# Half of an output projection moved from its own stage into the attention loop

## The chip, the core and the metric

The kernel runs on one core of a Trainium2 chip. Its time is the device time of one execution in microseconds; before the change it was 3228.24, 3230.65 and 3234.8 us in three runs, 3230.65 in the median. Five engines work side by side, each through its own queue in order: TensorE (PE, with the loading of its weights shown as PEld), VectorE (DVE), ScalarE (ACT), GpSimd (POOL) and SyncE (SP), which here issues nearly all transfers. Results of TensorE go to PSUM and are read from there by VectorE and ScalarE.

## What is computed

Two layers on `x` of 2 x 1024 tokens of width 512. The change concerns the first layer's attention, a gated delta rule with 16 heads of width 128, and above all its last line, the output projection with `Wo` of 2048 x 512:

```python
def step(S, inps):
    qt, kt, vt, at, bt = inps
    Sk = jnp.einsum('bhvk,bhk->bhv', S, kt)
    err = Sk - vt
    S = at[..., None, None] * S - bt[..., None, None] * (err[..., None] * kt[:, :, None, :])
    ot = jnp.einsum('bhvk,bhk->bhv', S, qt)
    return (S, ot)
...
o = (o - mu) * jax.lax.rsqrt(var + 1e-05) * ln_w + ln_b
g = jax.nn.sigmoid(x @ Wg).reshape(B, T, H, DV)
o = (o * g).reshape(B, T, H * DV)
return o @ Wo
```

Around it:

```python
xn = _layernorm(x, axis=-1)
s = _L0_attn_ref(xn, ...)
g = _silu(_L0_ffn_ref(xn, ...))
x = x + s * g
xn = _layernorm(x, axis=-1)
```

The second layer is a gated recurrence over the tokens and an MLP with packed 4-bit weights, which ends in another `x + s * g`. All products are in float32 or close to it.

## The kernel before, in words

Time goes through four stages. A front computes the first layernorm, the first MLP (its result `gd` goes to HBM) and prepares the keys of the first head groups (0 to 436 us). Then comes the **attention loop** (436 to about 1798 us), then the **join** (the rest of the output projection, the gate, the sum and the second layernorm, to 2024 us), then the second layer.

**The loop.** Tokens are cut into `NC` = 8 chunks of 128 and heads into `HG` = 8 groups of two; with both batch entries a group has `NS` = 4 streams. A unit is one chunk of one head group. `units` takes the groups in pairs: units 0 to 15 are groups 0 and 1 in turn, 16 to 31 groups 2 and 3, and so on to 63. So heads 0 to 7 are finished for all chunks soon after unit 31.

A unit's own work is a chain of short dependent steps. `across` solves a triangular system in four blocks: a product into `zw`, a copy (`w4`), four small transfers of 16 KB (`wt`), then the next block; at its end it updates the state (`pst`). `finish` makes the unit's output (`po`), normalises, gates it and stores it (`od<-ot`) in HBM. Beside the chain, `weave` hands out wide products in portions by their costs in `LINKS` = 10 links a unit. These are projections for later windows: `made` for queries, values and gates, and `ahead_k` for keys, three groups ahead. Each is eight products of 128x512 (`WIDE`). Chains of neighbouring units overlap: `weave` gets the chain of the unit before and that of this unit, and advances one in each link. `later(n, ...)` defers the steps that follow a product by n links.

With `turn4` = u % 4, a unit with turn4 2 or 3 carries two such projections. One with turn4 0 or 1 carries one and, while `slot + 3 < HG`, `ahead_k` as a second; from unit 40 on there are no keys left to make, and these are the light units.

**Order.** In the loop the compute engines keep the program's order (`Ordered`). The transfers on SP, and all that the join issues, are placed by a scheduler when the program is built. SP executes its queue in order, and a transfer that waits holds up those behind it.

**The join.** `Join` is made by `then()` at unit 48 (slot `HG - 2`), after the pools of the loop's key side are closed (`early`: `at_a`, `at_k`, `at_l`). Its constructor loads all of `Wo` in four transfers of 1 MB (L154). `order` lists the 16 tiles of 128 tokens by chunk, then batch entry; a tile is named by its place i there, 0 to 15. `load_o` (L174) loads a tile's heads, 1 MB, `load_xg` its `x` and `gd`. `product` multiplies the 16 heads into one PSUM tile `jpo`; `rest` gates it (L216), adds `x` (L212), stores it (`x1d`), takes statistics (L207 to L209), a power on GpSimd (L219) and normalises (L220). `turn` transposes the tile twice (`ptr`, L114), once into `xd` in HBM through ScalarE, once into the operand `xq` of the second layer through VectorE, with four differences for odd chunks.

Tiles 0 to 2 are multiplied in the loop's last two passes and after it. `run` makes the other 13: it starts a tile's product, turns the former tile after 8 of its 16 heads, and does the rest. The second layer's first weights are unpacked on VectorE in the same stretch, since the scheduler lets them in as soon as their room is free.

Of the kernel before, what the change touches and what calls it, by code (L numbers as in the profile page):

```python
# [13 lines left out]
F32 = mybir.dt.float32  # L14
# [4 lines left out]
ALU = mybir.AluOpType  # L19
# [3 lines left out]
P = 128  # L23
B, T, D = 2, 1024, 512
NT = B * T
KC = D // P
NTT = NT // P
H = 16
HG = H // 2
NC = T // P  # L30
NS = 4
# [32 lines left out]
def done(steps):  # L64
    for _ in steps:
        pass
# [56 lines left out]
class Ordered:  # L123


    def __init__(self, tc, engine, on):
        self.tc, self.engine, self.on = tc, engine, on
# [11 lines left out]
class Join:  # L139
# [1 line left out]

    def __init__(self, tc, a, cst, minus_half, od, gd, x1d):
        self.tc, self.a, self.cst, self.minus_half = tc, a, cst, minus_half
        self.od, self.gd, self.x1d = od, gd, x1d
        self.ctx = ExitStack()
        self.tp = [self.pool("j_t", 1)]
        wp, self.op = self.pool("j_w", 1), [self.pool("j_o", 1)]
        self.lp = self.pool("j_ln", 3)  # L150
        self.wo = []
        for h0 in range(0, H, 4):
            w = wp.tile([P, 4, D], F32, name=f"wo_{h0}")
            tc.nc.sync.dma_start(  # L154
                w, a["wo"][h0 * P : (h0 + 4) * P, :].rearrange("(h p) e -> p h e", p=P)
            )
            self.wo += [w[:, h, :] for h in range(4)]
        self.order = [(c, b) for c in range(NC) for b in range(B)]
        self.o, self.xg, self.made = [], [], 0
        self.load_xg()  # L160

    def pool(self, name, bufs):
        return self.ctx.enter_context(self.tc.tile_pool(name=name, bufs=bufs, reuse_waits="tile"))

    def more_room(self):
        self.tp.append(self.pool("j_t2", 2))
# [2 lines left out]
    def load_o(self):  # L169

        n = len(self.o)
        c, b = self.order[n]
        ot = self.op[n % 3 > 0].tile([P, H, P], F32, tag="ot", name=f"jo_{b * NC + c}")
        self.tc.nc.sync.dma_start(ot, self.od[c].rearrange("p (h b) t -> p b h t", b=B)[:, b])  # L174
        self.o.append(ot)

    def load_xg(self):
# [10 lines left out]
    def product(self, psp, tag, matmul):  # L188


        nc = self.tc.nc
        i = self.made
        self.made += 1
        c, b = self.order[i]
        ti = b * NC + c
        ot, (xt, g) = self.o[i], self.xg[i]
        po = psp.tile([P, D], F32, tag=tag, name=f"jpo_{ti}")
        for h in range(H):
            matmul(po, lhsT=ot[:, h, :], rhs=self.wo[h], start=(h == 0), stop=(h == H - 1))  # L199
            if h == H - 1:  # L200
                st, mv, ve, rs = (
                    self.lp.tile([P, n], F32, tag=f"ln_{t}", name=f"ln_{t}")
                    for t, n in (("st", 6), ("mv", 2), ("ve", 1), ("rs", 1))
                )

                def stats():
                    nc.vector.bn_stats(st, xt)  # L207
                    nc.vector.bn_aggr(mv, st)
                    nc.vector.tensor_scalar(ve, mv[:, 1:2], EPS, None, ALU.add)  # L209

                def added():
                    nc.vector.tensor_tensor(xt, g, xt, ALU.add)  # L212
                    nc.sync.dma_start(self.x1d[ti], xt)

                self.rest = lambda out=g: (
                    lambda: nc.vector.tensor_tensor(g, po, g, ALU.mult),  # L216
                    added,
                    stats,
                    lambda: nc.gpsimd.tensor_tensor(rs, ve, self.minus_half[:, 0:1], ALU.pow),  # L219
                    lambda: nc.vector.tensor_scalar(  # L220
                        out, xt, mv[:, 0:1], rs, ALU.subtract, ALU.mult
                    ),
                )
            yield WIDE

    def run(self, xd, xq, xp):

        nc, tc = self.tc.nc, self.tc
        with self.ctx as ctx:
            ps_o, ps_t = (  # L230
                ctx.enter_context(tc.tile_pool(name=n, bufs=bufs, space=PSUM, reuse_waits="tile"))
                for n, bufs in (("j_pso", 3), ("j_pst", 2))
            )
            late = None
            for i in range(NTT):
                if i >= self.made:
                    for _ in range(min(i + 3, NTT) - len(self.o)):
                        self.load_o()
                    product = self.product(ps_o, "pso", nc.tensor.matmul)
                    done(itertools.islice(product, H // 2))  # L240
                    if late is not None:
                        late(nc, ps_t, "pst", self.xg[i - 1][0].rearrange("p (k t) -> p k t", k=KC))
                    done(product)
                    g = self.xg[i][1]
                    if i == NTT - 1:
                        g = xp.tile([P, D], F32, name="xn_last")
                    for step in self.rest(g):
                        step()
                elif late is not None:
                    late(nc, ps_t, "pst", self.xg[i - 1][0].rearrange("p (k t) -> p k t", k=KC))  # L250
                if late is not None:
                    for _ in range(min(i + 3, NTT) - len(self.xg)):
                        self.load_xg()
                g = g if i == NTT - 1 else self.xg[i][1]
                late = functools.partial(self.turn, xd, xq, *self.order[i], g)
        return late
# [14 lines left out]


@with_exitstack
def first_layer(ctx, tc, a, cst, minus_half, keep, xnT, od, gd, then):

# [24 lines left out]
    nc = tc.nc  # L302
# [7 lines left out]
    pools = {}  # L310
# [215 lines left out]
    def later(n, *steps):  # L526


        for i, step in enumerate(steps):
            if order["loop"] and n + i:  # L530
                due.setdefault(order["slot"] + n + i, []).append(step)
            else:
                step()
# [85 lines left out]
    def ahead_k(hg, p, wk, store):  # L619
        ka = pa.tile([P, NS, 2 * P], F32, tag="ka", name=f"ka_{hg}_{p}")  # L620
        store["ka", p] = ka
        yield from project(1, "wk", hg, p, wk, ka)
        later(5, lambda: nc.sync.dma_start(store["k"][p], ka))
# [341 lines left out]
    with tc.issue_after(last["act"].ins):  # L965
# [3 lines left out]
        done(made(0, 0, "v"))  # L969
        done(made(1, 0, "q"))  # L970
        done(within(0, 0, stores[0]))
        def joined():

            for cost in joining.product(pools["a"], "pa", PE.matmul):
                yield cost
            later(1, *joining.rest())
# [3 lines left out]
        for u in range(len(units) + 1):  # L980
# [15 lines left out]
            if u % 8 == 0:  # L996
                steps = invert(slot + 2, stores[slot + 2]) if slot + 2 < HG else none
                if slot + 3 < HG:
                    wk = load_weights(slot + 3, ("wk",))
                    stores[slot + 3] = new_store(slot + 3)  # L1000
                if slot == HG - 2:
                    early.close()
                    joining = then()
            if u % 8 < 7:
                for k in (0, 2, 4, 5, 7, 9) if u % 8 else (0, 7, 8, 9):
                    later(k + 1, lambda steps=steps: next(steps, None))
            pot, late = late, none
            other(pot, 1, 8 * NARROW)
            later(8, lambda pot=pot: done(pot))
# [21 lines left out]
            if turn4 < 2:  # L1031
                if slot + 3 < HG and u < len(units):
                    tail = [(ahead_k(slot + 3, i, wk["wk"], stores[slot + 3]), 8 * WIDE)]
            elif turn4 == 2:
                if u < len(units):
                    tail = [(made(C, p, "gate"), 8 * WIDE)]
            elif p + 1 < NP:
                tail = [(made(C, p + 1, "q"), 8 * WIDE)]
            elif C + 2 < HG:
                tail = [(made(C + 2, 0, "q"), 8 * WIDE)]  # L1040
# [23 lines left out]
            for hg, n, when in (  # L1064
# [2 lines left out]
            ):  # L1067
                if at == when and hg < HG:
                    weights.setdefault(hg, {}).update(load_weights(hg, ("w" + n,)))
            if joining and at == 8:  # L1070
                joining.load_o()
            if u == len(units) - 2:

                last_w.close()
                joining.more_room()
                for _ in range(2):
                    joining.load_o()
                    joining.load_xg()
# [433 lines left out]
def body(ctx, tc, a, out):  # L1512
# [7 lines left out]
    od = [tc.dram_tile([P, H * B, P], F32, name=f"od_{c}") for c in range(NC)]  # L1520
    x1d = [tc.dram_tile([P, D], F32, name=f"x1d_{ti}") for ti in range(NTT)]
    xd = [tc.dram_tile([KC, P, T], F32, name=f"xd_{b}") for b in range(B)]

    xp = ctx.enter_context(ExitStack())

    xnT = xp.enter_context(tc.tile_pool(name="xn", bufs=1)).tile([P, KC, B, T], F32, name="xnT")
    joining = first_layer(
        tc, a, cst, minus_half, keep, xnT, od, gd, lambda: Join(tc, a, cst, minus_half, od, gd, x1d)
    )
    eo = ctx.enter_context(tc.tile_pool(name="eo", bufs=1, side="right", reuse_waits="tile"))  # L1530

# [78 lines left out]
```

## Time and profile before

| what | value |
|---|---|
| runs | 3228.24, 3230.65, 3234.8 us |
| profiled execution | 3230.2 us, span 3228.4 us, mean granted clock 0.994 |
| loop, unit 0 to the end of unit 62 | 436.5 to 1777.8 us |
| wide products in units 44 to 57 | 162 |
| output projection `jpo` | 256 products: 48 by L131 in and just after the loop, 208 by L199 |
| `wo` in 4 transfers | issued 1479.7 to 1489.6, 5.7 to 10.2 us to landing |
| `jo` in 16 transfers | 6.1 us to landing, median |
| `jx`, `jg`, `xd`, `x1d` in the join's steady part | 2.7, 3.0, 3.3, 5.2 us to landing |

A product of float32 is shown as two records, so 256 products are 512 records of `jpo`. In the profile `po<-w_d` belongs to the second layer. The rows of the profile quoted later name an engine, a line of the kernel, an operation and its output and inputs; in windows, each engine has its busy time and its count of instructions, and then follow the granted clock of TensorE as a share, the mean busy share of the 16 DMA engines and the rate in GB/s.

### The profile page before, as it was taken

What the parts mean: (1) busy time and instruction counts of PE and PEld (TensorE: products, weight loads), DVE (VectorE), ACT (ScalarE), POOL (GpSimd) and SP (SyncE); (2) the same over time, 40 slices, a digit from 0 to 9 for tenths busy, and PEclk for the clock granted to TensorE, in tenths of its full rate; (3) what the DMA queues carried; (4) which work ended last, traced back from release to release, by engine and by line L of the source; (5) the groups of instructions that cost most, each with busy time, mean ns of one, the idle gap of its engine ahead of it and who ended that gap; (6) DMA issues with size and microseconds to landing.
All of it is one profiled execution on the core that took longest, in us unless ns stands there. A gap on an engine that the chain in (4) does not pass through costs nothing.

```text
span 3228.4 us, 38168 instructions
## 1 busy us (share of the span) xinstructions
PE 3162.7 (98%) x12454; PEld 1958.0 (61%) x12454; DVE 2145.3 (66%) x4286; ACT 1245.8 (39%) x2259; POOL 829.7 (26%) x1204
## 2 busy tenths in 40 slices
PE   8999999999999999998999999999999999999998
PEld 6566756666666666665666544555555555555554
DVE  4566578686877877675655433676677666776677
ACT  3475445546555555444444100222222222322223
POOL 2000022322222232222332200333323332333322
PEclk9999999999999999999999999999999999999999
DMA  6244333444434443434323544111001010110014
GB/s 181 65 140 108 97 109 107 116 129 129 122 109 132 134 127 110 98 112 130 88 71 85 165 136 120 39 33 33 26 26 33 27 33 27 33 33 27 26 36 130
DMA packets 498246, 281.11 MB, mean 87 GB/s; under 512 B 206848, under 2 KB 443136, under 8 KB 498048
## 3 DMA queue, kind: packets, MB, share of 16 engines
q1 hardware_dynamic: 490048, 265.83, 29.3%
q0 software_dynamic: 5696, 8.65, 1.0%
q10 hardware_dynamic: 2304, 4.20, 0.4%
q8 instruction: 99, 1.62, 0.2%
q14 instruction: 99, 0.81, 0.1%
HBM read 179.71 MB, written 86.25 MB: 82 GB/s over the span
## 4 chain that ended last, share of the span: by engine, by line
PE 85%; DVE 5%; DMA 3%; issue 3%; ACT 2%; SPq 1%; POOL 1%; DVEq 0%; ACTq 0%; POOLq 0%
PE po L131 15%; PE pua L131 7%; PE pga L131 7%; PE pgate L131 6%; PE pwk L131 6%; PE pwq L131 5%; PE jpo L199 5%; PE pwv L131 4%; PE zw L131 4%; PE pgc L131 3%; PE puc L131 3%; PE pg L403 2%; PE pu L403 2%; PE po L426 2%; PE pub L131 2%
## 5 line engine op out<-in xcount | busy, mean ns | idle before, releaser
L131 DVE TENSOR_TENSOR acc<-acc,po 128x512 f32<-128x512 f32 x408 | 278.2, 682 | 208.3 <-PE po L131 207.6
L131 PEld LDWEIGHTS po<-w_d,i 128*128 128x128 f32 x1024 | 194.5, 190 | 142.6 <-issue 110.7
L131 PE MATMUL po<-w_d,i 128*128 128x256 f32 (+1 forms) x1024 | 275.3, 392 | 0.0
L131 PE MATMUL pgate<-xnT,wg 128*128 128x512 f32 x512 | 248.6, 595 | 0.0
L131 PE MATMUL pwv<-xnT,wv 128*128 128x512 f32 x512 | 245.0, 593 | 1.8 <-ACT gate L131 1.8
L131 PE MATMUL pwq<-xnT,wq 128*128 128x512 f32 x512 | 245.2, 593 | 0.0
L131 PE MATMUL pua<-xq,w_u 128*128 128x512 f32 x512 | 240.6, 592 | 0.0
L131 PE MATMUL pga<-xq,w_g 128*128 128x512 f32 x512 | 240.6, 592 | 0.0
L131 PE MATMUL pwk<-xnT,wk 128*128 128x512 f32 x512 | 236.8, 593 | 2.4 <-ACT ka L131 2.4
L131 ACT COPY g<-pga 128x512 f32<-128x512 f32 x96 | 56.2, 585 | 447.2 <-PE pga L131 440.0
L131 DVE SCALAR_TENSOR_TENSOR v<-prewv,cw,v 128x512 f32<-128x512 f32 x192 | 168.2, 877 | 64.6 <-ACT v L131 53.1
L131 PEld LDWEIGHTS po<-w_d,s 128*128 128x128 f32 x720 | 136.8, 190 | 95.4 <-issue 77.3
L131 PE MATMUL po<-w_d,s 128*128 128x256 f32 x720 | 184.8, 379 | 0.0
L199 PE MATMUL jpo<-wo,jo 128*128 128x512 f32 x416 | 182.9, 597 | 0.0
L131 ACT COPY w<-zw 128x128 f32<-128x128 f32 x192 | 50.6, 264 | 338.9 <-PE zw L131 338.6
L131 POOL TENSOR_TENSOR rs<-rs,minus_half 128x4 f32<-128x4 f32 x64 | 64.4, 1007 | 426.9 <-DVE rs L131 387.9
L131 DVE SCALAR_TENSOR_TENSOR ka<-prewk,cw,ka 128x512 f32<-128x512 f32 x192 | 148.1, 773 | 37.1 <-ACT ka L131 26.7
L131 PEld LDWEIGHTS zw<-rr,ground 128*128 128x128 f32 x512 | 97.1, 193 | 123.7 <-issue 98.0
L131 DVE TENSOR_TENSOR rr<-rr,zw 128x128 f32<-128x128 f32 x192 | 54.9, 286 | 175.8 <-PE zw L131 174.2
L131 DVE SCALAR_TENSOR_TENSOR q<-prewq,cw,q 128x512 f32<-128x512 f32 x192 | 159.3, 830 | 14.4 <-ACT q L131 8.0
L131 POOL TENSOR_TENSOR ot<-ot,gate 128x512 f32<-128x512 f32 x64 | 87.1, 1360 | 297.5 <-ACT ot L131 266.6
L131 ACT ACT_TABLE_LOAD x115 | 147.5, 1283 | 14.5 <-PE pr L131 11.3
(244 smaller groups left out, 6612.9 us busy)
## 6 DMA issues: line engine op xcount, KB each, us to landing
e<-gr SPq DMA_DIRECT2D x64, 256.0 KB, 4.1
de<-e SPq DMA_DIRECT2D x64, 256.0 KB, 2.7
dk<-ka SPq DMA_DIRECT2D x32, 512.0 KB, 2.8
kb<-dk SPq DMA_DIRECT2D x64, 256.0 KB, 3.5
eb<-de SPq DMA_DIRECT2D x64, 256.0 KB, 3.0
eg<-egr SPq DMA_DIRECT2D x64, 256.0 KB, 3.9
od<-ot SPq DMA_DIRECT2D x64, 256.0 KB, 2.1
jo<-od SPq DMA_DIRECT2D x16, 1024.0 KB, 6.1
```

Of the source, the lines that this page charges most:

```text
L131: i = getattr(self.engine, name)(*args, **kw)
L199: matmul(po, lhsT=ot[:, h, :], rhs=self.wo[h], start=(h == 0), stop=(h == H - 1))
L403: nc.tensor.matmul(pp, lhsT=mw[wt, ic][:, kc, :], rhs=part, start=(kc == 0 and i == 0), stop=(kc == KC - 1 and i == 1),)
L426: nc.tensor.matmul(po[tl], lhsT=part[:, tl * P : (tl + 1) * P], rhs=mw["dwT", ic - 1], start=(ic == 1 and i == 0), stop=(ic == IC and i == 1),
```

## The change

For 8 of the 16 tiles (4, 5, 7, 8, 10, 11, 12 and 13) the first eight heads are multiplied in the loop, in the second place of the light units 44, 45, 48, 49, 52, 53, 56 and 57. The eight heads' part of `Wo` is loaded in units 41 to 43 into buffers of the key side that are free by then (`woh`: two of tag `ka`, four of tag `e`). The tile's heads (`oh`, 512 KB) go into the key weights' buffer `wk`, one at a time, so that each load waits for the former half product. ScalarE copies the half product out of PSUM and SP stores it in HBM (`pd`). In the join such a tile loads its `pd` into the place of heads 0 to 3, multiplies only heads 8 to 15, and VectorE adds both before the gate.

The pools of the key side are now closed and `Join` is made at unit 58, and all of `Wo` is loaded there by `load_wo`, a quarter in each of units 58 to 61 by the program's order. The first tile's load moves to unit 61 in the program. In `run` the former tile is turned after the whole product, not in its middle, except for the last tile.

```diff
+    def load_wo(self):
+        h0 = len(self.wo)
+        w = self.wp.tile([P, 4, D], F32, name=f"wo_{h0}")
+        self.tc.nc.sync.dma_start(
+            w, self.a["wo"][h0 * P : (h0 + 4) * P, :].rearrange("(h p) e -> p h e", p=P)
+        )
+        self.wo += [w[:, h, :] for h in range(4)]
...
-        self.tc.nc.sync.dma_start(ot, self.od[c].rearrange("p (h b) t -> p b h t", b=B)[:, b])
+        h0 = 0
+        if n in self.pd:
+            h0 = H // 2
+            self.tc.nc.sync.dma_start(ot[:, 0:4], self.pd[n].rearrange("p (k t) -> p k t", k=4))
+        self.tc.nc.sync.dma_start(
+            ot[:, h0:], self.od[c].rearrange("p (h b) t -> p b h t", b=B)[:, b, h0:]
+        )
...
-        for h in range(H):
-            matmul(po, lhsT=ot[:, h, :], rhs=self.wo[h], start=(h == 0), stop=(h == H - 1))
+        h0 = H // 2 if i in self.pd else 0
+        for h in range(h0, H):
+            matmul(po, lhsT=ot[:, h, :], rhs=self.wo[h], start=(h == h0), stop=(h == H - 1))
...
+                def gated():
+                    total = po
+                    if h0:
+                        total = ot[:, 0:4].rearrange("p k t -> p (k t)")
+                        nc.vector.tensor_tensor(total, total, po, ALU.add)
+                    nc.vector.tensor_tensor(g, total, g, ALU.mult)
...
-                    done(itertools.islice(product, H // 2))
-                    if late is not None:
+                    if i == NTT - 1:
+                        done(itertools.islice(product, H // 2))
                         late(nc, ps_t, "pst", self.xg[i - 1][0].rearrange("p (k t) -> p k t", k=KC))
                     done(product)
...
-                elif late is not None:
+                if late is not None and (i < NTT - 1 or i < self.made - 1):
                     late(nc, ps_t, "pst", self.xg[i - 1][0].rearrange("p (k t) -> p k t", k=KC))
...
+            def load(cls):
+                c, b = halves[0] // B, halves[0] % B
+                o = kp.tile([P, KC, 2 * P], F32, tag="wk", name=f"oh_{halves[0]}")
+                cls.o = o.rearrange("p k (h t) -> p (k h) t", h=2)
+                nc.sync.dma_start(
+                    cls.o, od[c].rearrange("p (h b) t -> p b h t", b=B)[:, b, 0 : H // 2]
+                )
...
+            def product(cls):
+                i, o = halves.pop(0), cls.o
+                po = pools["a"].tile([P, D], F32, tag="pa", name=f"poh_{i}")
+
+                def out():
+                    part = pa.tile([P, NS, P], F32, tag="lt", name=f"part_{i}")
+                    part = part.rearrange("p s t -> p (s t)")
+                    ACT.copy(part, po)
+                    later(1, lambda: nc.sync.dma_start(pd[i], part))
+
+                for h in range(H // 2):
+                    mm(po, lhsT=o[:, h, :], rhs=cls.wo[h], start=(h == 0), stop=(h == H // 2 - 1))
+                    if h == H // 2 - 1:
+                        later(1, out)
+                    yield WIDE
...
-                if slot == HG - 2:
-                    early.close()
-                    joining = then()
...
+            if u == 58:
+                early.close()
+                joining = then()
+            if 58 <= u < 62:
+                joining.load_wo()
...
                 if slot + 3 < HG and u < len(units):
                     tail = [(ahead_k(slot + 3, i, wk["wk"], stores[slot + 3]), 8 * WIDE)]
+                elif u > 43 and halves:
+                    tail = [(half.product(), 8 * WIDE)]
...
-            if joining and at == 8:
+            if u == 61:
                 joining.load_o()
+            if u in (41, 42, 43):
+                half.more()
+            if u > 42 and halves and u % 4 in (0, 3):
+                half.load()
...
+    pd = {i: tc.dram_tile([P, D], F32, name=f"pd_{i}") for i in (4, 5, 7, 8, 10, 11, 12, 13)}
```

## The prediction

> **What bounds the kernel now.** I read the page first, then stretches of the attention loop and of the join, and only then single instructions.
>
> ```profile
> PE 3162.7 (98%) x12454; PEld 1958.0 (61%) x12454; DVE 2145.3 (66%) x4286; ACT 1245.8 (39%) x2259; POOL 829.7 (26%) x1204
> ```
>
> TensorE looks full, and the change takes no product away: it moves 64 of them. All depends on how much real idle time lies where they go, so that 98% has to be resolved. First the rate. In the join TensorE runs without a wait:
>
> ```profile
> 1912.85 1.08 PE L114 MATMUL ptr<-cst,jg 128*128 128x128 f32 x8
> ...
> 1913.76 13.90 PE L199 MATMUL jpo<-wo,jo 128*128 128x512 f32 x32
> ```
>
> 32 records in 13.90 us, of which the last lasts 0.59: one starts every 0.429 us. A float32 product of 128x512 is two records, 0.859 us; eight are 6.87, sixteen 13.74; the eight transposes of a turned tile take 0.91 (13.76 less 12.85). The 128x128 records start every 0.11 us (the 16 of `po` take 1.79 in the chain of waits). A record's own 0.59 us overlaps its follower, so busy time overstates the work; counts times rates don't.
>
> Units 44 to 57 of the loop (from the first `pr` of one to that of the next) and the join after it:
>
> ```profile
> core 0: us, PE busy (x) PEld busy (x) DVE busy (x) ACT busy (x) POOL busy (x), PEclk, DMA share, GB/s
> 1412.70:1687.40 274.70, 258.96 (x1285) 175.42 (x1286) 163.96 (x430) 114.14 (x240) 80.62 (x123) 0.97 0.37 102
> ...
> 1823.70:2023.80 200.10, 195.67 (x542) 93.67 (x540) 76.08 (x160) 11.14 (x19) 19.77 (x26) 0.98 0.48 143
> ```
>
> ```profile
> L131 PE MATMUL pgate<-xnT,wg 128*128 128x512 f32 x112 | 55.6, 601 | 0.0
> L131 PE MATMUL pwv<-xnT,wv 128*128 128x512 f32 x108 | 52.6, 593 | 0.0
> L131 PE MATMUL pwq<-xnT,wq 128*128 128x512 f32 x104 | 48.9, 593 | 0.0
> ```
>
> The groups by shape give 324 wide records in the loop's stretch; the other 961 are narrow. Work: 324 x 0.429 + 961 x 0.11 = 244.7 us of 274.7, so **30 us are really lost**, though the profile shows only 15.7 idle. For the join: 418 x 0.429 + 124 x 0.11 = 193 of 200.1, 7 lost.
>
> Where the 30 lie:
>
> ```profile
> 1491.00:1514.80 23.80, 16.81 (x73) 11.11 (x72) 12.78 (x37) 8.49 (x17) 5.40 (x10) 0.87 0.62 197
> ...
> 1573.10:1592.10 19.00, 17.18 (x88) 12.74 (x89) 13.57 (x39) 8.04 (x16) 6.20 (x9) 0.91 0.49 139
> 1592.10:1608.70 16.60, 16.60 (x93) 11.77 (x92) 6.71 (x27) 5.97 (x14) 5.85 (x7) 1.00 0.35 97
> ```
>
> ```profile
> 1579.66 1.02 PE L131 MATMUL pwv<-xnT,wv 128*128 128x512 f32 x2
> 1582.50 1.47 PE L131 MATMUL pst<-wt,kd 128*128 128x128 f32 x8 [1.81 <-DVE wt L131]
> ```
>
> Units come in fours: u%4 of 0 and 1 are light (no `ahead_k` from unit 40 on), 2 and 3 full. Unit 52 (the window from 1573.10) does 14.8 us of work in 19.0: `pst` waits for the chain of `wt`, which takes 9.4 us from the unit's start, and the clock falls (0.91). But unit 53 (from 1592.10), light too, has 16.5 of work in 16.6: **nothing to fill**. Counted alike, units 44, 48, 52 and 56 lose 4.5, 10.8, 4.2 and 4.2; 45, 49, 53 and 57 lose 0.9, 0.4, 0.1 and 0.1; the six full ones 4.8. Unit 48 is worse because the four 1 MB loads of `wo` are issued just before it (the last lands after 10.2 us).
>
> **The change, part by part.**
>
> *64 products enter units 44 to 57.* +64 x 0.859 = +55.0 us. They take over the idle time as far as the chain finishes behind them. In the built order six of the eight stand ahead of `pst` (5.2 us), against a wait of 1.8 and a chain that was 9.4 long beside 7.6 of work: room for 3 us of further delay. The nearest row for what remains are the units up to 39, which carry `ahead_k`: unit 24 fills its 21.8 us, clock 1.00, and by the same count units 18 to 31 lose 4.3 us together. So 30 falls to 4: **+29** net. Ends: +25 (nothing lost) and +36 (a third of the idle time stays).
>
> Here a rule differs from the row. The Trainium skill (TensorE: Matmul & The Clock Gate, Part 1) has the clock halved after about 3.4 us without activity. Unit 52 shows no gap above 1.81 us, yet its clock is 0.91, some 1.7 us lost; over the stretch 3% of 274.7, 8 us. By the rule waits this short cost only themselves, filling recovers the 15.7 recorded, and the stretch grows by 39. I take the row: the clock is back to 1.00 where units are full.
>
> *Transfers.* SP gets 30 more: six `woh`, eight `oh` (512 KB), eight stores of `pd`, eight loads of `pd`. A 1 MB `jo` load took 0.53 to issue and 6.1 to land, so 0.55 and about 4 for an `oh`. An `oh` waits on SP for the former half product, and `wt` transfers stand behind it; but in TensorE's order that product ends ahead of the `zw` from whose copy those `wt` come, so the wait is over by then; the `wt` land 2 to 4 us later, within the room above. The store of `pd` waits for ScalarE, with `eb` and `kb` of the next unit behind it, about a unit early. ScalarE's eight copies (0.585 each by `g<-pga`) go to an engine busy 114 of 274.7 us. Nothing, ends 0 and +10.
>
> *The `wo` loads* leave unit 48 (its excess is in the 30) and stand, in the built order, from the end of unit 57 through 58. A 1 MB `jo` load at the end of unit 51 left units 51 and 52 losing as much as 55 and 56, which have none. +1, ends 0 and +4. Unit 60 stays unfilled.
>
> *64 products leave the join.* -55.0. A half tile takes 6.87 + 0.91 = 7.78 instead of 14.65. What else must fit:
>
> ```profile
> 1906.18 0.69 DVE L216 TENSOR_TENSOR jg<-jpo,jg 128x512 f32<-128x512 f32 x1 [4.59 <-PE jpo L199]
> ...
> 1909.51 0.55 DVE L220 TENSOR_SCALAR jg<-jx,ln_mv,ln_rs 128x512 f32<-128x512 f32 x1 [0.73 <-POOL ln_rs L219]
> ```
>
> The chain from product to transposes takes 4.0. The added sum is one more 128x512 (0.69, with its gap 0.77): 4.8. VectorE's order puts the former turn into it: one copy (0.77) and for odd c four differences (0.42 each, one beside GpSimd's power): 7.0. The turn now stands behind the whole next product, so 7.8 are there. TensorE stays the bound, with 0.8 to spare. Transfers: about 1.8 MB a half tile, 230 GB/s; the join's loads run near 300 at their peaks. SP's longest wait, `jx` for the landing of `xd` (3.4), ends about 6 us after a product.
>
> *The join's first tiles* don't fit. VectorE unpacks the second layer's first weights from 1838.5, in one queue with the tiles' sums; that costs 4.3 us of wait now, and 2.6 at half clock after it. With half products, tile 3's product ends at 1839.6, tile 4's at 1847.3; tile 3's sum stands behind 5.8 us of unpacking and is turned at 1850.5 (wait 3.2); tile 4's stands behind 5 more, is done at 1862.4 and is wanted at 1858.5 (wait 3.9). With a cold clock after each, 10.5 against 7: +3.5, ends 0 and +8. Join: **-51.5**, ends -55 and -43.
>
> Sum: +29 + 1 - 51.5 = -21.5. From the profiled execution's 3230.2 (span 3228.4; the median is 3230.65, 0.5 above) that gives **3209**.
>
> **The rivals.**
>
> *Only the recorded idle time is filled*: +39 in the loop, -11 in all, **3219**. For it: the rule above, and SP's tight issue of `wt` (0.58 each). Against it: the full units.
>
> *The join gives it back*: the half tile's chain is over 7.8, say 10 with the transfers' help, and the eight tiles lose 2.2 each and some clock: join -32, in all about -2, **3228**. For it: 0.8 us of room only, a sum of 1.21 us where transfers are dense (at 1845.8). Against: the chain's steady 4.0.
>
> *Slower: the loads hold up the chain.* SP is one queue in order. If `oh` delays the `wt` behind it as `wo` did in unit 48 (landing 9.8 us instead of 1.8), a half unit loses up to 10.8 - 4.2 = 6.6. From 2.7 us in each of the eight the gain is gone; at 4.5 it is +14.5, **3245**. For it: unit 48. Against: that was four times 1 MB at once; one `oh` is an eighth of it, and units before 40 ran at 0.5 to 0.6 DMA share without loss.
>
> *Better*: the join's start stalls no more than now and the loop keeps 2 us: -27, **3203**.
>
> That the products are not moved is excluded by the built order: eight wide products stand in each of the eight units.
>
> **How the numbers follow.** Forecast 0.62, recorded idle only 0.13, join gives back 0.08, loads 0.06, better 0.11. Bounds: +25 - 55 = -30 and +36 + 4 - 43 = -3; a range that leaves out 2 in 10 is 3200 to 3223. A measurement tells apart about 0.2%, 6.5 us. Faster by more: 0.62 + 0.13 + 0.11 and a little of the rest, 0.87; within 0.2%: 0.07; slower: 0.06.
>
> **What would show it.** Right: units 44, 48, 52 and 56 near 21.7 us (48 about 20) at clock 1.00, their light neighbours near 23.4 (49 near 22.5); units 44 to 57 together 304; half tiles in the join 7.8 apart; the join 148 to 149 long; two waits of `ptr` for `jg` within its first 40 us. Wrong: `pst` or `poh` waiting for DMA in the half units; waits of `ptr` at every half tile; new losses in units 58 to 61.

## The result and the profile after

The changed kernel takes 3206.22 us in the median of six runs (3205.01 to 3208.78); the kernel before, beside it, took 3230.25 (3228.11 to 3234.8). The ratio is 0.9925, with an interval from 0.9912 to 0.9938. The profiled execution took 3207.82 us, with a span of 3206.0, 22.4 less than the span before.

The first row of the page hardly differs, as it must when no product is taken away: the same 12454 records, and eight instructions more each on VectorE (the sums of two halves) and ScalarE (the copies).

```profile
PE 3154.4 (98%) x12454; PEld 1953.3 (61%) x12454; DVE 2145.9 (67%) x4294; ACT 1249.3 (39%) x2267; POOL 829.2 (26%) x1204
```

What changed is in the stages. This table cuts both kernels at the same instructions: units at their first `pr`, the join from the first `ptr` to the last `jpo`, and "rest" is the second layer. Both kernels were profiled a second time later ("again").

| stage, us | before | before, again | after | after, again |
|---|---|---|---|---|
| front, up to unit 0 | 436.5 | 438.9 | 440.4 | 439.8 |
| units 0 to 39 | 895.3 | 896.3 | 897.3 | 897.3 |
| units 40 to 43 | 80.9 | 78.6 | 82.1 | 82.3 |
| units 44 to 57 | 274.7 | 272.4 | 304.7 | 304.7 |
| unit 58 to the join | 136.6 | 136.6 | 136.0 | 136.0 |
| join | 199.3 | 197.2 | 140.7 | 143.0 |
| rest | 1205.2 | 1205.0 | 1204.8 | 1204.7 |

The two stages of the change gained 28.6 in the first pair (474.0 to 445.4) and 21.9 in the second. The first pair's span shows 22.4, since the front and the units up to 43 took 7.1 longer there and the remaining stages 1.0 less.

The windows view of the changed kernel, for the loop's stretch and the join (columns as before: start and end, length, then busy time and count of each engine, granted clock, share of the DMA engines, GB/s):

```profile
core 0: us, PE busy (x) PEld busy (x) DVE busy (x) ACT busy (x) POOL busy (x), PEclk, DMA share, GB/s
1419.80:1724.50 304.70, 302.12 (x1410) 192.12 (x1409) 160.54 (x430) 117.54 (x248) 79.94 (x124) 1.00 0.36 98
1860.50:2001.20 140.70, 137.53 (x409) 67.27 (x408) 74.66 (x168) 11.14 (x19) 20.22 (x26) 1.00 0.63 191
```

The stretch grew by 30. Its clock rose from 0.97 to 1.00 and its recorded idle time fell from 15.7 to 2.6. All 64 half products (`poh`) stand in it, but two other products (`pwv`, 108 records before) have slipped into unit 43, ahead of it:

```profile
L131 PE MATMUL poh<-woh,oh 128*128 128x512 f32 x128 | 60.2, 593 | 0.0
...
L131 PE MATMUL pwv<-xnT,wv 128*128 128x512 f32 x105 | 49.5, 593 | 0.0
```

One of the 105 only ends in the stretch, so 448 wide records start there, 124 more than before: 53.2 us of work. By the prediction's own count, 304.7 - 244.7 - 53.2 = 6.8 us are still lost where it was 30. The units tell where:

```profile
1419.80:1443.70 23.90, 22.76 (x105) 14.13 (x104) 18.97 (x54) 8.32 (x17) 6.15 (x8) 1.00 0.42 120
1443.70:1465.50 21.80, 21.80 (x106) 14.05 (x105) 8.01 (x32) 7.55 (x17) 4.87 (x7) 1.00 0.57 164
1508.50:1529.00 20.50, 20.29 (x89) 12.21 (x88) 11.50 (x35) 8.73 (x18) 7.51 (x11) 1.00 0.47 121
1593.00:1615.00 22.00, 22.00 (x106) 14.22 (x105) 12.85 (x38) 8.07 (x17) 7.13 (x11) 1.00 0.48 139
1615.00:1636.70 21.70, 21.70 (x105) 14.03 (x104) 6.36 (x24) 6.47 (x15) 4.41 (x6) 1.00 0.43 125
```

These are units 44, 45, 48, 52 and 53. Unit 52 went from 19.0 to 22.0: it took in 16 records, 6.87 us of work, for 3.0. Unit 53 took in 12, 5.15 us of work, and went from 16.6 to 21.75: it paid the full price. The first was partly empty, the second was not. The remaining four of a pair's 32 records stand in the full unit before it, as wide work now starts earlier. Only unit 44 still has a noticeable idle stretch.

The waits view of TensorE over the same stretch (what waits, for what, then us in all, times, and the longest) names hardly anything, and no transfer at all:

```profile
PE zw L131 <- ACT w L131: 1.3, 2, 1.1
PE pst L131 <- DVE wt L131: 0.7, 1, 0.7
PE zw L131 <- DVE rr L131: 0.3, 1, 0.3
```

Before, transfers were named here:

```profile
PE pst L131 <- DMA ground<-dl: 4.0, 2, 2.2
...
PE pk L131 <- DMA kb<-dk: 2.6, 1, 2.6
```

In the join, VectorE's timeline shows two half tiles in the steady part (columns: start, duration, engine, line, operation, output and inputs, and in brackets the idle time before it and what ended it):

```profile
1948.10 0.69 DVE L230 TENSOR_TENSOR jo<-jo,jpo 128x512 f32<-128x512 f32 x1 [3.42 <-PE jpo L210]
...
1952.58 0.55 DVE L238 TENSOR_SCALAR jg<-jx,ln_mv,ln_rs 128x512 f32<-128x512 f32 x1 [0.73 <-POOL ln_rs L237]
...
1955.89 0.69 DVE L230 TENSOR_TENSOR jo<-jo,jpo 128x512 f32<-128x512 f32 x1 [2.77 <-PE jpo L210]
```

L230 is the added sum of the two halves. It starts every 7.79 us, when TensorE has finished a half product, and VectorE idles about 3 us each time. TensorE stays the bound, and its waits in the join are two, both at the start:

```profile
PE ptr L114 <- DVE jg L238: 2.7, 1, 2.7
PE ptr L114 <- DVE sp_e L99: 0.5, 1, 0.5
```

### The profile page after: what moved, and what is told of

Same layout as the page of the kernel before. It is cut to its first block, busy times and chain, and to the rows that moved or that the text cites. A ratio compares the mean times of both kernels' runs of the same rounds, so it can differ in the third digit from the quotient of the medians.

```text
span 3206.0 us, 38256 instructions
## 1 busy us (share of the span) xinstructions
PE 3154.4 (98%) x12454; PEld 1953.3 (61%) x12454; DVE 2145.9 (67%) x4294; ACT 1249.3 (39%) x2267; POOL 829.2 (26%) x1204
## 4 chain that ended last, share of the span: by engine, by line
PE 87%; DVE 5%; DMA 3%; ACT 2%; issue 2%; SPq 1%; POOL 0%; DVEq 0%; ACTq 0%; POOLq 0%
PE po L131 15%; PE pua L131 7%; PE pga L131 7%; PE pgate L131 6%; PE pwk L131 6%; PE pwq L131 5%; PE pwv L131 5%; PE zw L131 4%; PE pgc L131 3%; PE puc L131 3%; PE jpo L210 3%; PE pg L423 2%; PE pu L423 2%; PE po L446 2%; PE pub L131 2%
## 5 line engine op out<-in xcount | busy, mean ns | idle before, releaser
L131 ACT ACT_TABLE_LOAD x115 | 147.5, 1283 | 14.5 <-PE pr L131 11.3
L131 PEld LDWEIGHTS zw<-w,ground 128*128 128x128 f32 x768 | 111.3, 192 | 65.7 <-issue 54.4
```

What stands on the lines that cost most here:

```text
L131: i = getattr(self.engine, name)(*args, **kw)
```

## The experiments

The theory on trial is the prediction's: what is gained is real idle time that the half products fill, and only the first light unit of each pair (44, 48, 52, 56) has any. The rivals: the gain comes from the change's other two edits, the later place of the `wo` loads or of the former tile's turn; or any light unit would do. All edits are against the changed kernel. Times are medians, with the ratio to the kernel before run on the same chip. The stages of two executions of one kernel differ by 2 to 3 us, as the table shows.

**No half products: the `wo` loads away from unit 48, the turn in its new place.**

```diff
-            if u in (41, 42, 43):
-                half.more()
...
-    pd = {i: tc.dram_tile([P, D], F32, name=f"pd_{i}") for i in (4, 5, 7, 8, 10, 11, 12, 13)}
+    pd = {i: tc.dram_tile([P, D], F32, name=f"pd_{i}") for i in ()}
```

> The change without half products: no tile has its first eight heads made in the loop, no woh, oh or pd transfers; only the later closing of the key side's pools, the wo loads at units 58 to 61 and the turn after the whole product are left. Theory (the products fill idle time): only the excess of unit 48 goes. Units 48 to 51 lost 12.8 us before and units 52 to 55 5.9, so -7 in the loop, units 44 to 57 near 268 us, the join near 199 as before: 3223. Rival (the gain is the wo loads' place): nearly all of the -24 is here, 3207. Rival (wo costs in its new place what it did in the old one): 3230.

It took 3218.04 us, ratio 0.9968 (0.9956 to 0.998): part of the gain is there with no half product moved. Its windows for units 44 to 57 and the join:

```profile
1415.20:1683.20 268.00, 254.79 (x1284) 172.37 (x1285) 163.81 (x430) 114.36 (x240) 81.15 (x123) 0.98 0.38 104
1819.20:2011.30 192.10, 192.10 (x537) 91.78 (x536) 70.45 (x160) 11.15 (x19) 19.63 (x26) 1.00 0.49 149
```

The program's order has the `wo` loads in units 58 to 61 here too, but the scheduler issued them in units 50 and 51 (1531.0 to 1551.9 us). With half products they are issued from the end of unit 57 to unit 59 (1722.7 to 1748.7 in the changed kernel). So this run shows what leaving unit 48 is worth, and not what the new place costs.

The loop is as expected. The join was expected unchanged, near 199, and took 192.1: TensorE is busy in every instant of it. So the turn's place, in which I had seen only room, might be worth 7 us by itself.

**The same, with the turn back in the middle of the product.** In `run`:

```diff
-                    if i == NTT - 1:
-                        done(itertools.islice(product, H // 2))
+                    done(itertools.islice(product, H // 2))
+                    if late is not None:
                         late(nc, ps_t, "pst", self.xg[i - 1][0].rearrange("p (k t) -> p k t", k=KC))
                     done(product)
...
-                if late is not None and (i < NTT - 1 or i < self.made - 1):
+                elif late is not None:
```

> The kernel wo_moved (no half products) with the former tile turned in the middle of a product again, as before the change: only the later closing of the pools and the place of the wo loads are left. wo_moved took 268.0 us in units 44 to 57 (6.7 less than before) and 192.1 in the join (7.2 less). Theory: the join's 7.2 come from the turn's new place, behind the whole product, which gives tile 3's sums the time that the unpacking of weights takes on VectorE: here the join is near 199 again, the loop stays at 268, and the time is near 3224. Rival: the join's gain comes from elsewhere (the wo loads' place, a warmer clock), then it stays near 192 and the time at 3218.

3227.03 us, ratio 0.9978 (0.9969 to 0.9986); loop 270.7, join 199.6. The join is back where it was. TensorE's timeline says why. With the turn in the middle:

```profile
1839.44 6.17 PE L210 MATMUL jpo<-wo,jo 128*128 128x512 f32 x14
...
1849.71 1.94 PE L114 MATMUL ptr<-cst,jg 128*128 128x128 f32 x8 [4.11 <-DVE jg L238]
```

With the turn after the product:

```profile
1835.78 13.90 PE L210 MATMUL jpo<-wo,jo 128*128 128x512 f32 x32
1849.52 1.08 PE L114 MATMUL ptr<-cst,jg 128*128 128x128 f32 x8
```

At the join's start VectorE is late with `jg`, as it unpacks weights. In the middle of the product, its transposes wait 4.11 us, and then run at half clock (1.94 for eight instead of 1.08). A whole product fills that time. By the stages the turn is worth 7.5 us to full tiles, or 5.1 against the second execution of the kernel before (197.2), which was at half clock for 3.4 us in the join where this one was for 6.8. The medians, each measured beside other runs of the kernel before, differ by 9.0, the ratios only by 0.001, which is 3 us; so the stages carry the size, and the timeline the cause.

The two kernels also bracket the `wo` loads. Between executions whose clock in units 52 and 56 is alike, the loop went from 272.4 to 268.0 and from 274.7 to 270.7: **4 us** for taking the loads out of unit 48's neighbourhood (unit 48: 23.8 to 20.1). The edit `wo_at_once` below tests their new place.

**The turn in the middle, with the half products.** The same edit of `run`, and nothing else.

> The whole change, but in the join a full tile turns the former tile in its middle again, as before; half tiles are unchanged by it (their eight products are all ahead of the turn). Theory: TensorE bounds the join and the chain of tile 5 and of tile 8 (7.0 us at most) just fits into eight products (6.9) and the turn of 0.9 ahead of them, so the same time within 2 us, 3206, join 141 to 143 us. Rival (the turn's new place is needed): three full tiles that follow half ones wait some 2 us each, 3212.

3206.79 us, ratio 0.9934 (0.9919 to 0.9948), join 142.1 against 140.7 and 143.0. Once half tiles stand in the join, the turn's place is worth nothing that can be told. Three transposes wait, 4.6 us in all, for the two waits of 3.2 above.

**Half products in the first light units only, or in the second only.** Four tiles each, 4, 7, 10 and 12:

```diff
-                elif u > 43 and halves:
+                elif u > 43 and turn4 == 0 and halves:
...
-            if u > 42 and halves and u % 4 in (0, 3):
+            if u > 42 and halves and u % 4 == 3:
...
-    pd = {i: tc.dram_tile([P, D], F32, name=f"pd_{i}") for i in (4, 5, 7, 8, 10, 11, 12, 13)}
+    pd = {i: tc.dram_tile([P, D], F32, name=f"pd_{i}") for i in (4, 7, 10, 12)}
```

The second version has `turn4 == 1` and `u % 4 == 0`.

> Only four tiles (4, 7, 10, 12), all in the first light unit of each four (44, 48, 52, 56); units 45, 49, 53 and 57 stay unfilled. Theory (time is gained only where TensorE was idle, which is in the first light units): 32 products enter (+27.5) and some 25 us of loss go, units 44 to 57 near 277 us; the join loses 27.5 and 2 to 3 of its waits, near 169 us. About the time of the whole change, 3206 (3203 to 3209), though half the products are moved. Rival (each product moved gains alike): half of what the eight tiles gain beyond the wo loads, about 3215.

> Only four tiles (4, 7, 10, 12), all in the second light unit of each four (45, 49, 53, 57), which had no idle time. Theory: +27.5 in the loop less the 7 us of the wo loads and 1 of small gaps, units 44 to 57 near 294 us; the join -27.5 and 2 to 3 of its waits, near 169 us. So the products bring almost nothing and the time is 3220, near that of the kernel with only the wo loads moved. Rival (each product moved gains alike): about 3215.

First units: 3198.6 us, ratio 0.991 (0.9894 to 0.9927). Second units: 3214.37 us, ratio 0.9957 (0.9942 to 0.9972). Their windows over units 44 to 57 and the join, the first units':

```profile
1411.10:1688.50 277.40, 274.78 (x1345) 179.96 (x1344) 162.06 (x429) 115.47 (x244) 79.83 (x123) 1.00 0.36 98
1825.10:1990.20 165.10, 164.88 (x474) 79.56 (x473) 72.05 (x164) 11.15 (x19) 19.95 (x26) 1.00 0.55 169
```

and the second units':

```profile
1414.80:1709.60 294.80, 281.85 (x1349) 184.69 (x1350) 161.08 (x430) 116.57 (x244) 81.25 (x124) 0.98 0.33 91
1845.60:2010.20 164.60, 164.60 (x473) 79.59 (x472) 72.03 (x164) 11.15 (x19) 19.96 (x26) 1.00 0.55 169
```

The join is the same in both: it gives back 27 us for 32 products. The loop isn't. Against 268.0 without half products, the first units take them for 9.4 us, the second for 26.8, nearly their whole 27.5. Loop and join together: 460.1 without half products, 442.5 with the first four, 459.4 with the second four, 445.4 with all eight. So the first four are worth 17.6, the second four nothing (0.7 alone, -2.9 on top of the first). This is the theory's central claim, and it holds; that any light unit would do is out.

The times themselves were not as expected. Both joins are 4 us shorter than the forecast, which had nothing for the turn's place, and the first version's front is short too (435.2). The second version's 3214.37 is even the number of the rival in which every product gains alike. But the kernel without half products took 3218.04 on that chip, not the 3223 that the forecast counted from: by the medians the second four gain 3.7 us, which is within the spread of the runs, and the first four 19.4.

**The same pair again**, beside both kernels:

> The kernel before once more, for its stages. The front before unit 0, which the change doesn't touch, took 436.5 us in the kernel before and 440.4 in the changed one, and 435.2 to 440.9 in the experiments; it holds stretches of 3.4 to 13.7 us at half clock near 340 us. Theory (where the clock falls is a matter of the execution): the front is anywhere from 435 to 441 here, the other stages as before within 2 us, units 44 to 57 near 275, join near 199. Rival (the program fixes it): 436.5 again.

> The whole change once more, beside first_light_again on one chip. Units 44 to 57 near 304.7, join near 140.7, time 3206; the front anywhere from 435 to 441 if it is a matter of the execution, 440.4 if the program fixes it.

> The kernel with half products in the first light units alone, beside the whole change on one chip. By the stages that the change touches (units 44 to 57 and the join) it was 2.9 us shorter, 442.5 against 445.4, but 7.6 by the medians. Theory: 3 us are the products' doing (tile 5 is whole, so tile 4's turn doesn't wait), the rest is the front's clock: between 3 and 8 less than the whole change, front anywhere from 435 to 441.

The kernel before gave 1.0005 of itself (0.9996 to 1.0013), so a tenth of a per cent can be told here. The changed one took 3208.28 us, 0.9938 (0.9923 to 0.9953), the one with the first light units 3198.57, 0.9908 (0.9893 to 0.9923): 9.7 us faster with half as many products moved, where 3 to 8 were expected. Their profiled executions are 7.5 apart: loop and join make 5.7 of it (447.7 against 442.0) and the front 3.6, while units 0 to 39 took 1.3 more.

**A fifth half product, in unit 40.** On top of the first-light version, tile 13 in unit 40, with `Wo`'s heads loaded in units 38 and 39 instead of 41 to 43, and each tile's heads from unit 39 on (not shown):

```diff
-                elif u > 43 and halves:
+                elif u > 39 and turn4 == 0 and halves:
...
-            if u in (41, 42, 43):
+            if u in (38, 39):
                 half.more()
...
-    pd = {i: tc.dram_tile([P, D], F32, name=f"pd_{i}") for i in (4, 5, 7, 8, 10, 11, 12, 13)}
+    pd = {i: tc.dram_tile([P, D], F32, name=f"pd_{i}") for i in (4, 7, 10, 12, 13)}
```

> The kernel first_light with a fifth half product (tile 13) in unit 40, whose eight heads of Wo are loaded in units 38 and 39. Unit 40 lost 6.6 us in every run. Theory: the product fills them, so units 40 to 43 take about 81 us as they did, while the join loses another 6.9 (158 us): 6 less than first_light, near 3193. Rival: the six loads of Wo (2 MB) and the tile's heads fall into unit 40 itself and hold up its chain, so that units 40 to 43 grow by 5 to 7 and the time stays near 3198.

3197.88 us, ratio 0.9882 (0.9865 to 0.9898), the lowest ratio of all. The join fell to 158.0, 7 us less, but units 40 to 43 took 84.5 instead of 79.8 to 82.0, and unit 39, which got four of the 16 records, 22.7 instead of 21.0. Unit 40 filled only in part:

```profile
1336.70:1361.10 24.40, 21.96 (x101) 14.39 (x100) 12.20 (x37) 7.80 (x17) 5.25 (x9) 0.93 0.50 114
```

It still idles 2.4 us, at clock 0.93. By the stages the fifth half product gained 2.3 us against the one execution with four and 0.6 against the other, not 6; the medians don't tell it from the version with four. The forecast had unit 40 losing 6.6 us in every run; by the count it loses 3.7 to 7.0, and 4.5 with the half product in it.

**All of `wo` at once, at unit 58.**

```diff
             if u == 58:
                 early.close()
                 joining = then()
-            if 58 <= u < 62:
-                joining.load_wo()
+                for _ in range(4):
+                    joining.load_wo()
```

> The whole change with all four wo loads issued at unit 58 by the program instead of a quarter in each of units 58 to 61. Theory: in a full unit the chain has room, and the built order had put all four between units 57 and 58 anyway: units 58 to 63 and the time the same within 2 us, 3206. Rival: what cost unit 48 was four loads at once, so units 57 to 59 lose 5 to 7 us, 3212.

The four loads are issued within 2.1 us (1719.9 to 1722.0), where the changed kernel's are spread over 26: the two orders do differ, which the theory denied. 3213.85 us, ratio 0.9932 (0.9917 to 0.9947). Unit 58 took 23.9 instead of 21.75:

```profile
1721.70:1745.70 24.00, 22.06 (x106) 14.01 (x105) 10.69 (x30) 9.36 (x19) 4.84 (x7) 1.00 0.69 235
```

The DMA share stands at 0.69, and TensorE idles 1.9. The stage up to the join grew by 2.9. So four loads together do hold up a chain, for about half of the 6 us that the rival gave, and spreading them avoids it. The medians don't tell the two apart with certainty.

**The unpacking moved behind tile 5's normalisation**, by an order between instructions of VectorE:

```diff
+    with tc.issue_after(mark.ins):
+        done(group_weights(0, weights))
-    done(group_weights(0, weights))
```

(`mark` is tile 5's last step; the bias's softplus is put behind it too.)

> The whole change, with the second layer's first unpacking of weights on VectorE put behind tile 5's sums in that engine's queue. Theory: the two waits of the join's start (0.6 and 2.9 us, 3.5 in all) are tile 3's and tile 4's sums behind the unpacking, so they go: join 137 to 138 us instead of 140.7, the loop as it was, the time 3 less than the whole change. Rival: something else starts too late (the sums themselves, transfers), then the join stays at 140.7 or moves its wait to tile 6 or to the second layer's first products.

3205.18 us, ratio 0.9908 (0.9894 to 0.9923), join 139.2. The waits at the start are gone. What is left is one wait, at a later tile:

```profile
PE ptr L114 <- DVE jg L238: 1.8, 1, 1.8
```

The unpacking has to be done somewhere in this queue; about 1.5 us was gained, less than forecast, and within what executions differ by.

## Why the prediction was right

**The loop, +30 with the `wo` loads: measured +30.0 and +32.3.** The account by counts and rates carried it: 30 us of lost time where the record of busy time showed 15.7. The rival in which only the recorded idle time is filled, +39 for the loop, is out. That the sum hit the 30.0 so closely is in part luck: 53.2 us of work came in instead of 55.0, and 6.8 us stayed lost instead of 4 and 1. Units 48, 52 and 56 came out at 20.5, 22.0 and 22.0 against 20, 21.7 and 21.7. Unit 44 took 23.9 and loses 2.3 us by the count. The second light units took 21.75 to 21.8, not 23.4, and unit 49 20.85 instead of 22.5: the prediction gave each 16 records, and they took in 12. The others went to the full units before, so 47, 51 and 55 took 3.3 us more in all, and 43 took 0.6 more.

**Row against rule.** The Trainium skill (TensorE: Matmul & The Clock Gate, Part 1) needs some 3.4 us of idleness for the clock to fall; the trace showed it low after 1.81. In the changed kernel the stretch is at 1.00 throughout, as the row had it. Yet the row isn't a rule either: the last section shows what the traces have in common.

**The `wo` loads.** I had counted all of unit 48's excess, near 7 us, as theirs. They account for 4. What remains there is the chain's own wait, `zw` for `rr`, 4.2 us without half products. The half product filled it all the same, so the sum wasn't hurt. Their new place costs nothing: unit 58 to the join took 0.6 less, against the forecast +1.

**Transfers.** TensorE waits for no `oh` or `pd` in the loop. An `oh` landed after 5.2 us in the median, not 4, and on SP's queue `wt` transfers waited three times for an `oh`, 2.1 us in all, by the profile; the room was enough for that. The slower rival is out.

**The join, -51.5: measured -58.6 and -54.2.** The 55.0 and the 7.78 a half tile are confirmed (7.79), so it does not give the gain back. The mis-sized term is "the first tiles, +3.5", 10.5 us lost there against 7. By the same count the join lost 4.0 us in the one execution and 6.2 in the other, against 7.6 and 5.5 in those of the kernel before: a gain in the first pair, next to nothing in the second. The waits were 0.5 and 2.7, in the other execution 1.0 and 2.7, not 3.2 and 3.9, and the clock was at half for 3.4 us in the other execution alone. VectorE at tile 3 shows why its wait was shorter. Its sum starts at 1878.92, as foreseen behind 5.75 us of unpacking:

```profile
1873.17 0.43 DVE L131 TENSOR_SCALAR hi_g<-pk_g 128x512 int32<-128x512 int32 x1 [1.43 <-DMA pk_g<-in_gpk]
...
1878.92 0.68 DVE L231 TENSOR_TENSOR jg<-jpo,jg 128x512 f32<-128x512 f32 x1
1879.52 0.68 DVE L120 COPY xq<-ptr 128x512 f32<-128x512 f32 x1
1880.12 0.70 DVE L223 TENSOR_TENSOR jx<-jg,jx 128x512 f32<-128x512 f32 x1
...
1883.86 0.55 DVE L238 TENSOR_SCALAR jg<-jx,ln_mv,ln_rs 128x512 f32<-128x512 f32 x1 [0.45 <-POOL ln_rs L237]
```

But from there to the end of the normalisation it takes 5.5, where the prediction's times leave 6.2 (a sum at 1844.3, turned at 1850.5). The kernel before took 7.3, as steps of the unpacking (the `hi_u` here is one) stood between its own:

```profile
1838.52 0.43 DVE L131 TENSOR_SCALAR hi_g<-pk_g 128x512 int32<-128x512 int32 x1 [0.60 <-DMA pk_g<-in_gpk]
...
1844.26 0.68 DVE L216 TENSOR_TENSOR jg<-jpo,jg 128x512 f32<-128x512 f32 x1
...
1844.93 0.96 DVE L131 TENSOR_SCALAR hi_u<-pk_u 128x512 int32<-128x512 int32 x1
...
1850.63 0.94 DVE L220 TENSOR_SCALAR jg<-jx,ln_mv,ln_rs 128x512 f32<-128x512 f32 x1 [0.45 <-POOL ln_rs L219]
```

In the changed kernel the scheduler had put them behind. The unpacking also began 12.7 us after the join's start at 1860.48, where before it began 14.5 us after 1823.98. These two make up most of the difference between a wait of 3.2 and one of 0.5.

The turn's new place was the other part that I undervalued. To full tiles it was worth 5 to 7.5 us by itself, but the half tiles bring some of the wait back: 192.1 less 55.0 would be 137.1, and the join took 140.7. With half tiles, the turn's place makes no measurable difference.

**What I did not forecast: the front and early loop.** Up to unit 44 the changed kernel took 7.1 more in the first pair and 5.6 more in the second. Only 0.6 of it is moved work, the two products in unit 43; unit 40 varies from 18.5 to 21.7 us between executions of kernels that put nothing there. This ate what the join gave beyond the forecast. The sum of -21.5 stands beside a measured difference in medians of 24.0 and, in the second pair, 20.3. It is right, but with two errors of opposite sign in it: that they nearly cancel is luck.

Of the 28.6 us in the two stages, about 4 come from where `wo` is loaded, 7.5 from the turn after a whole product, 14.7 from the half products, of which the first light units bring all. That is 26.2; the other 2.4 are mostly the clock of units 52 and 56 in that execution of the kernel before. In the second pair the 21.9 us divide into 4.4, 5.1 and 12.4. The front takes some of it back. The versions with four and five half products in the first light units only, at 3198.6 and 3197.9, beat both kernels.

## What to carry to other kernels

Where float32 matmuls overlap in the record, count records and multiply by the start-to-start rate: on a page that said "98% busy", a stretch of 275 us had lost 30, of which the record of busy time showed 15.7. Move work only into stretches that this count shows to be partly empty; half of what was moved here went where nothing was free, cost as much as it saved, and made a later tile wait. Put the step that waits for a slow chain behind a whole product rather than in its middle, before moving any work to hide that wait.

## What the runs showed of the hardware

**After a wait of 1.8 us the clock halves in one execution and not in another.** In unit 52 `pst` waits for `wt` in both executions of the kernel before, 1.81 us each time. In the first the clock was then at half for 3.4 us and the unit took 19.0. In the second it wasn't:

```profile
1574.20:1592.00 17.80, 15.76 (x88) 11.24 (x89) 13.61 (x39) 8.04 (x16) 6.19 (x9) 1.00 0.48 135
```

Same instructions, same wait, clock 1.00, 17.75 us. Unit 56 does the same (18.95 and 17.76). So a wait of this length costs itself and sometimes 1.2 us more.

The traces show much of what decides. In each of the 13 traces, the stretches at half clock (but for the last one, at the kernel's end) last 3.41 us or a multiple of it, and they all start on one grid of 3.41 us. These are windows of that grid around the wait in unit 52, two in the first execution and then three in the second:

```profile
1580.39:1583.80 3.41, 1.59 (x10) 1.23 (x10) 3.22 (x7) 1.52 (x3) 3.20 (x4) 1.00 0.22 41
1583.81:1587.22 3.41, 3.41 (x18) 3.25 (x17) 3.31 (x9) 0.27 (x1) 0.10 (x1) 0.50 0.38 105
...
1579.23:1582.64 3.41, 2.60 (x11) 1.23 (x9) 2.16 (x2) 2.61 (x5) 2.85 (x3) 1.00 0.12 29
1582.64:1586.05 3.41, 2.23 (x15) 1.92 (x16) 3.22 (x9) 0.55 (x1) 2.09 (x4) 1.00 0.39 77
1586.05:1589.47 3.42, 3.42 (x33) 3.42 (x32) 3.35 (x8) 0.77 (x2) 0.10 (x1) 1.00 0.22 72
```

In the first, the whole wait falls into one window; in the second, two windows share it. The 13 traces have some 12000 such windows at full clock after the first 14 us. The next window was at half clock after none of those with less than 1.5 us of recorded idle time, after all 51 with 1.9 us or more, and after 17 of the 38 in between. So what counts here is the idle time within a window, not the length of a wait. 1.81 us lies in the undecided middle: in unit 56 of the second execution it fell into one window too, and the clock stayed. The 2.69 us wait in the changed kernel's join was split into 1.1 and 1.6 in the one execution, and nothing followed; in the other it was split into 0.6 and 2.1, and 3.4 us at half clock followed.

**The front is not the same in kernels that differ only later.** It took 439.8 to 440.9 us in the five profiles of kernels with eight half tiles, 435.2 and 436.2 in the two with four in the first light units, and 436.5 to 438.9 in the other six. In all of the first five TensorE waits 2.4 to 3.3 us for `hl` near 336 us; in the other eight it waits 0.9 to 1.3. In the changed kernel half clock then stands for 13.7 us (0.79 from 320 to 350 us), in the two profiles of the kernel before for 3.4 and 10.2. Wait and clock explain most of it. Why the wait is longer is open: no run was made that changes only this.
